# Seven products interleaved over two halves, sums left to adding transfers, and an operation's stated time changed

## The chip, the cores and the metric

The kernel runs on one core of one Trainium2 chip. The metric is the time of one execution on the device in microseconds: the median of three runs is 2280.56 us (2279.93 to 2280.93). One further execution was recorded by the hardware profiler. TensorE (PE) multiplies matrices and writes into banks of PSUM. VectorE (DVE) and ScalarE (ACT) read those banks and the on-chip memory (SBUF). GpSimd (POOL) does small work and can issue transfers (DMAs), as SyncE (SP) and ACT can.

## The reference, cut to what matters

`x` has 128 graphs of 64 nodes with 256 features, 8192 rows in all, and `adj` is 64 x 64. Four layers follow each other, each with a residual and a layer norm. The change lies in the first and in what the second needs of `adj`:

```
def layer0(x, adj, W1, W2, W3):              # 256 -> 512 -> 1024 -> 256
    conv = lambda x, W: einsum('nm,bmh->bnh', adj * adj, einsum('bnf,fh->bnh', x, W))
    return conv(relu(conv(relu(conv(x, W1)), W2)), W3)
def layer1(x, adj, W1, b1, W2, b2):
    deg = sum(adj, 0) + sum(adj, 1) - diagonal(adj)
    d = where(deg > 0, rsqrt(deg), 0)
    _, U = eigh(d[:, None] * (diag(deg) - adj) * d[None, :])
    h = relu(einsum('mn,bnd->bmd', U.T, x) @ W1 + b1)
    return einsum('nm,bmd->bnd', U, h @ W2 + b2)
x = layernorm(x + layer0(x))      # then layer1, an LSTM layer (layer 2), an attention layer (layer 3)
```

The eigenvectors U of a 64 x 64 matrix have to be there before layer 1 begins.

## The kernel before, in words

**Groups.** The rows are worked on in 16 groups of four tiles of 128 rows; `order` (L892) names which group comes when. For a group, `burst` (L1025) multiplies by adj * adj in 64 small matmuls of 64 x 64, and ACT copies the two banks out (L1037). `weigh` (L1103) multiplies one tile by the first weight into one bank, and ACT applies relu into h1. Two more bursts turn h1 into m2, and m2 times the second weight gives h2 (relu). h2 times the third weight gives s3; `mix_rows` (L1108) applies adj * adj to s3 and adds the rows x, and seven pieces of a norm per pair of tiles are queued and taken one by one at later steps.

**Seven products.** A product with the second or the third weight is split in two by two blocks and done by seven half-size products instead of eight (Winograd's form). `seven` (L1058) runs them in the order 1, 2, 6, 5, 7, 3, 4: 1, 6, 7 and 4 accumulate in one PSUM bank (`ch`), 2 in a bank of its own (`ps`), 5 and 3 in a third (`b5`). After a product ACT copies, or DVE adds and ACT applies relu, into a quarter of h2 or s3, and the next product into the same bank has to wait for that read. `step` (L1007) delays this work by one product in the written order. The products need sums of blocks of both operands. Those of the weights are made once (`sums_of_weights`, four DVE operations each). Those of m2 are made for each group by `sums_second` (L1121, four DVE operations of 128x512). Those of h2 are made by four DVE operations of 128x1024 in each group (the `VL.tensor_add` and `VL.tensor_sub` lines of `layer0`): two write the tile sh, two overwrite parts of h2. The second weight is worked off in two halves, j = 0 and j = 1, one after the other, with the next group's first burst between them. The last two groups (`PLAIN = 2`) multiply by the third weight directly (`plain`, L1093).

**Eigenvectors.** `eigen` (L275) is a Python generator that computes U beside layer 0, nearly all of it on DVE with operations of at most 64 x 64. It reduces the matrix to three diagonals in 62 steps (L382 on). Each step has some 24 DVE operations, a copy on ACT (L385), a square root on ACT (L397), and one matmul (L312), which needs DVE's copy into the tile LV, and whose result (the PSUM tile pa) DVE needs at once. Then it finds the eigenvalues by bisection (six passes, tiles Q and br, `V.least = 0.285`), evaluates continuants (tile D2, 63 pairs of operations on tw and D, `V.least = 0.22`), forms the vectors, transposes them on TensorE (L644), fixes their signs, multiplies with the reduction's matrix (pa<-AQ,Z) and lays U and its transpose out twice as u2 and ut2.

**What sets the order.** In layer 0, PE, DVE and ACT carry out instructions in the order in which Python emits them. A clock `now` advances with every matmul by its stated time. `between` (L955), called after each matmul, resumes `eigen` when `now` has reached the time that it last yielded. That time comes from `Timed` (L42), which adds a stated time for each DVE operation: `least` and 0.0009 us for each element over 64. `least` is 0.25 unless set. `soon()` asks for a return a little before DVE is free, `full()`, ahead of a matmul, at the time when it is. So stated times decide where an eigenvector matmul stands among layer 0's matmuls. What is left of `eigen` when layer 0 has been emitted is emitted at its end. Layers 1 to 3 are recorded and ordered by a planner of their own (`Plan`, shown by the profile as L162); their weights are loaded by SP into memory that layer 0 leaves.

Of the kernel before, what the change touches and what calls it, by code (L numbers as in the profile page):

```python
# [41 lines left out]
class Timed:  # L42
# [3 lines left out]
    def __init__(self, engine, free, until):  # L46
        self.engine, self.free, self.until, self.least = engine, free, until, 0.25

# [226 lines left out]
def eigen(tc, stack, a, ident, cst, u2, ut2, now, free):  # L275
# [21 lines left out]
    def ps(shape, tag):  # L297
        uid[0] += 1
        return pp.tile(shape, F32, tag=tag, name=f"{tag}_{uid[0]}")
# [5 lines left out]
    def soon():  # L305
        return max(free[0], until[0]) - 0.45

    def full(turns=0):
        return max(free[0], until[0]) + 0.6 * turns

    def mm(out, lhsT, rhs):
        PE.matmul(out, lhsT, rhs, start=True, stop=True)  # L312
        now[0] += 0.2
        until[0] = now[0] + 0.5
# [161 lines left out]
    def rows(col, n, tag):  # L476
        b = sb([N, N], "bc")
        V.tensor_scalar(b, C["ones"], col, None, op0=ALU.mult)
        yield full()
        p = ps([N, n, N], tag)  # L480
        mm(p, b, cst[:N, 0:n, :])
        return p
# [76 lines left out]
    M = cp.tile([W, FAN, HALF], F32, name="M")  # L559
    V.least = 0.285  # L560
    yield soon()
# [39 lines left out]
    V.tensor_copy(D2[:, N - 1:], dl[:, 0:1])  # L601
    V.least = 0.22
    for k in range(1, N):
# [4 lines left out]
        yield soon()  # L608
    V.least = 0.25
    D = cp.tile([N, 2, N], F32, name="D")  # L610
# [94 lines left out]
    pl = (yield from rows(lam, 1, "pa"))[:, 0, :]  # L705
    V.tensor_scalar(t0, pl, lam, 1e-12, op0=ALU.subtract, op1=ALU.add)
    V.reciprocal(t0, t0)
    V.tensor_mul(t0, t0, C["off"])
    V.tensor_copy(t1, pl)
    V.tensor_mul(t1, t1, t1)  # L710
    V.tensor_reduce(co_[8], t1, AX.X, ALU.max)
    V.tensor_scalar(co_[8], co_[8], nrm, (8.0 * 2.0 ** -24) ** 2, op0=ALU.mult, op1=ALU.mult)
    pp_ = (yield from rows(co_[7], 1, "pa"))[:, 0, :]
    rowdot(hs, pp_, t0)
    V.tensor_scalar(hs, hs, -1.0, 1.0, op0=ALU.mult, op1=ALU.add)
    V.tensor_mul(hs, hs, hs)
    V.tensor_mul(hs, hs, co_[8])
    yield soon()
    V.tensor_scalar(co_[9], s1, s1, 2.0, op0=ALU.mult, op1=ALU.mult)
    V.tensor_tensor(co_[9], co_[9], hs, ALU.is_gt)  # L720
    V.tensor_scalar(co_[10], s2e, s2e, 2.0, op0=ALU.mult, op1=ALU.mult)
    V.tensor_tensor(co_[10], co_[10], co_[8], ALU.is_gt)
    yield soon()
    V.tensor_scalar(co_[11], s2e, 0.0, -2.0, op0=ALU.is_gt, op1=ALU.mult)
    V.tensor_scalar(co_[11], co_[11], co_[10], 1.0, op0=ALU.mult, op1=ALU.add)
    V.tensor_scalar(co_[12], s1, 0.0, -2.0, op0=ALU.is_gt, op1=ALU.mult)
    V.tensor_scalar(co_[12], co_[12], 1.0, co_[11], op0=ALU.add, op1=ALU.subtract)
    V.tensor_scalar(co_[12], co_[12], co_[9], co_[11], op0=ALU.mult, op1=ALU.add)
    V.tensor_mul(co_[12], co_[12], rn)

# [4 lines left out]
    UT = cp.tile([N, N], F32, name="UT")  # L735
    V.tensor_scalar(UT, pu, co_[12], None, op0=ALU.mult)
    yield full()
    pt = ps([N, N], "pa")
    PE.transpose(pt, UT, C["eye"])
    until[0] = now[0] + 0.7  # L740
    U = cp.tile([N, N], F32, name="U")
    V.tensor_copy(U, pt)
    V.memset(u2, 0.0)
    V.memset(ut2, 0.0)
    yield full()
    for out, lhsT in ((u2, UT), (ut2, U)):
        p2 = ps([2 * N, N], "pa")
        for h in range(2):
            mm(p2[h * N:(h + 1) * N, :], lhsT, C["eye"])
        for h in range(2):  # L750
            V.tensor_copy(out[h * N:(h + 1) * N, h * N:(h + 1) * N], p2[h * N:(h + 1) * N, :])

# [19 lines left out]
QUADS = 1.17  # L772
PLAIN = 2

# [56 lines left out]
def kernel(  # L831
# [32 lines left out]
    def tl(pool, shape, tag, **kw):  # L864
        uid[0] += 1
        return pool.tile(shape, F32, tag=tag, name=f"{tag}_{uid[0]}", **kw)
# [110 lines left out]
    def quads(c):  # L977
        for m in (slice(0, N), slice(N, P)):
            for h, hs in enumerate((slice(0, N), slice(N, P))):
# [5 lines left out]
    D11, D12, D21, D22 = (aw3[:, r:r + 4, c:c + P] for r in (0, 4) for c in (0, P))  # L985
    tv = wa.tile([P, 4, 4, P], F32, name="tv")
    m1 = pa.tile([P, 2, 512], F32, name="m1")
    h1 = pa.tile([P, 4, 512], F32, name="h1")
    m2 = pa.tile([P, 4, 512], F32, name="m2")
    ss = pa.tile([P, 3, 2, 256], F32, name="ss")  # L990
    h2 = pa.tile([P, 8, 512], F32, name="h2")
    sh = pa.tile([P, 2, 4, 256], F32, name="sh")
    s3 = pa.tile([P, 4, D], F32, name="s3")
    A11, A12, A21, A22 = (m2[:, k:k + 2, r:r + 256] for r in (0, 256) for k in (0, 2))
    H11, H12, H21, H22 = (h2[:, c:c + 4, r:r + 256] for r in (0, 256) for c in (0, 4))


    second = ((None, B11, B21, B22, tw[:, 2], B12, tw[:, 1], tw[:, 0]),
              (None, A11, A12, ss[:, 2], A22, ss[:, 0], ss[:, 1], A21))
    third = ((None, D11, D21, D22, tv[:, 2], tv[:, 3], tv[:, 1], tv[:, 0]),  # L1000
             (None, H11, H12, H12, H22, sh[:, 0], sh[:, 1], H21))
    free = [0.0]
    VL = Timed(V, free, now)
    spare = [lambda: tl(pa, [P, D], "spare")]
    pending = []
# [10 lines left out]
    def bank(tag="ps"):  # L1016
        return tl(psa, [P, 512], tag, bufs={"ps": 4, "ch": 2, "b5": 1}[tag])

    def sums_of_weights(w, b12):
        VL.tensor_sub(w[7], w[3], b12)  # L1020
        VL.tensor_sub(w[5], b12, w[1])
        VL.tensor_sub(w[6], w[3], w[5])
        VL.tensor_sub(w[4], w[2], w[6])

    def burst(dst, src, c):  # L1025
# [31 lines left out]

    def seven(n, product, c11, c12, c21, c22, last):  # L1058

        def view(b):  # L1060
            return b[:, :2 * n].rearrange("p (i n) -> p i n", i=2)

        def add(dst, b):
            VL.tensor_add(dst, dst, b)
            if last is relu:
                relu(dst, dst)

        ch = view(bank("ch"))
        product(ch, 1, True)
        step(lambda: S.copy(c11, ch))  # L1070
        yield
        b2 = view(bank())
        product(b2, 2, True)
        step(lambda: add(c11, b2))
        yield
        product(ch, 6, False)
        step(lambda: S.copy(c12, ch))  # L1077
        yield
        b5 = view(bank("b5"))
        product(b5, 5, True)  # L1080
        step(lambda: S.copy(c22, b5))
        yield
        product(ch, 7, False)
        step(lambda: add(c22, ch))
        yield
        product(b5, 3, False)
        step(lambda: add(c12, b5))
        yield
        product(ch, 4, False)
        step(lambda: last(c21, ch))  # L1090
        yield

    def plain():  # L1093
        for t in (0, 2):
            p = bank().rearrange("p (t f) -> p t f", t=2)
            for i in range(2):
                run(p[:, i, :], [(h2[:, c, (t + i) * P:(t + i + 1) * P], aw3[:, c, :]) for c in range(8)])
                step((lambda p=p, t=t: S.copy(s3[:, t:t + 2, :], p)) if i else None)
                yield
        for _ in range(3):  # L1100
            yield
# [26 lines left out]
    def layer0():  # L1128
        n = NT // 4
        burst(m1, rows_of(order[0]), 0)  # L1130
        step()
        for t in range(4):
            weigh(t)
        step()
        sums_of_weights(second[0], B12)
        for c in (0, 2):
            burst(m2, h1, c)
        step()
        for g in range(n):
            sums_second()  # L1140
            for j in range(2):
                q = [h2[:, 4 * c + 2 * j:4 * c + 2 * j + 2, r:r + 256] for r in (0, 256) for c in (0, 1)]
                for _ in seven(256, by_second(j), *q, relu):
                    pass
                if j == 0 and g + 1 < n:
                    burst(m1, rows_of(order[g + 1]), 0)
                if j == g == 0:
                    sums_of_weights(third[0], D12)
            q = [s3[:, r:r + 2, c:c + P] for r in (0, 2) for c in (0, P)]
            w3 = seven(P, by_third, *q, S.copy) if g < n - PLAIN else plain()  # L1150
            next(w3)
            next(w3)
            if g < n - PLAIN:
                VL.tensor_add(sh[:, 0], H21, H22)
                VL.tensor_sub(sh[:, 1], sh[:, 0], H11)
            for t in range(4):
                if g + 1 < n:
                    weigh(t)
                if t == 0 and g < n - PLAIN:
                    VL.tensor_sub(H21, H11, H21)  # L1160
                    VL.tensor_sub(H12, H12, sh[:, 1])
            for _ in range(4):
                next(w3)
            if g + 1 < n:
                burst(m2, h1, 0)
            next(w3)
            if g + 1 < n:
                burst(m2, h1, 2)
            for t in (0, 2):
                mix_rows(g, t)  # L1170
        step()
# [657 lines left out]
```

## Time and profile before

| | |
|---|---|
| median of three runs | 2280.56 us |
| the profiled execution, its own time | 2277.23 us |
| its span, first to last instruction | 2275.4 us |
| TensorE busy (share of the span) | 2233.0 us (98%) |
| DVE busy | 1772.5 us (78%) |
| ACT busy | 1189.5 us (52%) |
| GpSimd busy | 137.0 us (6%) |
| layer 0, to its last matmul | 828.2 us |
| one group in layer 0 | about 49 to 50.5 us |
| DVE busy in layer 0, 310 to 360 us | 39.1 of 50 us |
| ACT busy there | 22.4 of 50 us |

A line of a timeline gives the start and the duration in us, the engine, the source line, the operation, out<-in by the program's names, and how many follow each other; in brackets stands how long the engine was idle before it and what ended that. A matmul of the program is two records in float32. A line of windows gives for a stretch each engine's busy time with its count, and at its end the TensorE clock granted (1.00 is full), the mean load of the 16 DMA engines, and GB/s.

### The profile page before, as it was taken

The page shows a single profiled execution, that of the slowest core. Times are in us where ns is not written, and L with a number is a line of the kernel's source. Part 1 is how long each engine was busy: PE and PEld are TensorE (multiplying, and loading weights), DVE is VectorE, ACT ScalarE, POOL GpSimd, SP SyncE. Part 2 cuts the span into 40 slices and gives each one's busy share as a digit, 9 for nine tenths or more (in the row PEclk, how much of TensorE's full clock was granted, in tenths as well). Part 3 has the DMA queues.
Part 4 walks back from the last instruction along what each step waited for, and adds up shares of the span by engine and source line. Part 5 has one row for each costly group of instructions (what it writes and reads, how often), then busy time and mean ns, then how long its engine had stood idle before and what let it go on. Part 6 is the DMA issues. An engine that isn't in the chain of part 4 may idle for free.

```text
span 2275.4 us, 52244 instructions
## 1 busy us (share of the span) xinstructions
PE 2233.0 (98%) x20612; PEld 1990.8 (87%) x20612; DVE 1772.5 (78%) x5868; ACT 1189.5 (52%) x2892; POOL 137.0 (6%) x315
## 2 busy tenths in 40 slices
PE   8999999999999989999999999999999999999997
PEld 6888888887788778999999999999999999999985
DVE  5888777776888879765967977977877887578977
ACT  3444444443434435665655655655656555566554
POOL 0000000000000010000100000000010010000012
PEclk9999999999999999999999999999999999999999
DMA  7000000000000031000111211211221211001331
GB/s 245 11 11 11 11 11 11 11 20 11 11 11 1 1 126 57 11 11 20 66 40 48 78 57 50 87 57 41 87 66 40 78 66 39 31 21 65 117 107 59
DMA packets 80117, 107.93 MB, mean 47 GB/s; under 512 B 23296, under 2 KB 64256, under 8 KB 79872
## 3 DMA queue, kind: packets, MB, share of 16 engines
q1 hardware_dynamic: 79520, 104.32, 14.1%
q8 instruction: 162, 2.65, 0.5%
q14 instruction: 83, 0.68, 0.1%
q10 hardware_dynamic: 352, 0.28, 0.0%
HBM read 57.64 MB, written 45.09 MB: 45 GB/s over the span
## 4 chain that ended last, share of the span: by engine, by line
PE 91%; DVE 6%; issue 1%; ACT 1%; DMA 1%; POOL 0%; SPq 0%; ACTq 0%; DVEq 0%; POOLq 0%
PE ps L162 58%; PE ch L966 14%; PE ps L966 10%; PE b L966 7%; PE ps L1031 2%; PE pa L312 1%; DVE w L162 1%; DVE D L52 1%; DVE tw L52 1%; DVE X L162 1%; DVE gates L162 0%; DVE st L162 0%; DVE v L162 0%; ACT gates L162 0%; DVE h L52 0%
## 5 line engine op out<-in xcount | busy, mean ns | idle before, releaser
L162 PE MATMUL ps<-w,wih 128*128 128x128 f32 (+2 forms) x2944 | 572.0, 298 | 0.3 <-ACT gates L162 0.3
L162 PE MATMUL ps<-w,sums 128*128 128x128 f32 (+2 forms) x3104 | 476.3, 293 | 0.1
L162 PEld LDWEIGHTS ps<-w,wih 128*128 128x128 f32 x2944 | 453.1, 191 | 26.5 <-issue 6.8
L162 PEld LDWEIGHTS ps<-w,sums 128*128 128x128 f32 x3104 | 422.7, 191 | 14.3 <-ACT gates L162 1.9
L162 ACT ACTIVATE gates<-gates,cbi 128x256 f32<-128x256 f32 (+4 forms) x736 | 314.0, 479 | 171.8 <-DVE gates L162 169.9
L162 DVE TENSOR_TENSOR gates<-gates,ps 128x512 f32<-128x512 f32 (+4 forms) x408 | 233.7, 583 | 171.1 <-PE ps L162 158.0
L162 ACT COPY gates<-ps 128x512 f32<-128x512 f32 (+4 forms) x408 | 204.2, 506 | 252.3 <-PE ps L162 245.4
L162 PE MATMUL ps<-hs,whh 128*128 128x128 f32 (+1 forms) x896 | 181.2, 284 | 0.1
L162 PE MATMUL ps<-w,whh 128*128 128x128 f32 (+1 forms) x896 | 181.2, 284 | 0.0
L162 ACT ACTIVATE gates<-ps,cbi 128x128 f32<-128x128 f32 (+2 forms) x368 | 119.5, 384 | 42.9 <-PE ps L162 42.5
L162 PEld LDWEIGHTS ps<-hs,whh 128*128 128x128 f32 x896 | 139.8, 191 | 0.3 <-DVE hs L162 0.3
L162 PEld LDWEIGHTS ps<-w,whh 128*128 128x128 f32 x896 | 139.8, 191 | 0.0
L975 ACT ACTIVATE h<-h 128x512 f32<-128x512 f32 x96 | 60.5, 630 | 150.9 <-DVE h L52 150.9
L966 PE MATMUL ch<-m,tw 128*128 128x256 f32 x512 | 124.7, 381 | 3.1 <-ACT h L1077 1.7
L966 PE MATMUL b<-ss,aw 128*128 128x256 f32 x512 | 121.9, 379 | 0.0
L966 PE MATMUL ps<-aw,m 128*128 128x512 f32 x256 | 116.0, 606 | 1.5 <-DMA aw<-in_a_w_dram 1.5
L966 PEld LDWEIGHTS ch<-m,tw 128*128 128x128 f32 x512 | 94.9, 190 | 18.6 <-DVE h L52 3.4
L966 PEld LDWEIGHTS b<-ss,aw 128*128 128x128 f32 x512 | 96.8, 190 | 12.9
L162 POOL TENSOR_SCALAR rs<-mv 128x2 f32<-128x2 f32 x96 | 23.5, 255 | 1325.1 <-DVE mv L162 1323.7
L966 PEld LDWEIGHTS ps<-aw,m 128*128 128x128 f32 x256 | 48.3, 194 | 55.7 <-issue 51.4
L1037 ACT COPY m<-ps 128x512 f32<-128x512 f32 x96 | 51.2, 587 | 75.5 <-PE ps L1031 75.0
L162 PE MATMUL ps<-hs,sums 128*128 128x128 f32 (+1 forms) x448 | 90.6, 284 | 0.0
(373 smaller groups left out, 4139.2 us busy)
## 6 DMA issues: line engine op xcount, KB each, us to landing
far<-w SPq DMA_DIRECT2D x42, 512.0 KB, 2.9
w<-far SPq DMA_DIRECT2D x168, 128.0 KB, 3.1
X<-rest SPq DMA_DIRECT2D x24, 512.0 KB, 3.3
out_dram<-X SPq DMA_DIRECT2D x64, 128.0 KB, 1.8
rest<-XA SPq DMA_DIRECT2D x12, 512.0 KB, 2.6
rest<-X SPq DMA_DIRECT2D x12, 512.0 KB, 2.8
XA<-in_x_dram SPq DMA_DIRECT2D x22, 256.0 KB, 6.9
aw<-in_a_w_dram SPq DMA_DIRECT2D x3, 1024.0 KB, 10.2
```

Source lines behind the costliest of these rows:

```text
L52: return getattr(self.engine, name)(out, *args, **kw)
L162: getattr(e, name)(*[real(x) for x in args], **{k: real(v) for k, v in kw.items()})
L312: PE.matmul(out, lhsT, rhs, start=True, stop=True)
L966: PE.matmul(out, lhsT, rhs, start=start, stop=stop, **kw)
L975: S.activation(dst, src, AF.Relu)
L1031: PE.matmul(p[h][m, k, t, :], src[hs, t, f], sqT2[hs, hs], start=True, stop=True)
L1037: S.copy(to[:, h, c:c + 2], p[h])
```

## The change

In the second weight, the two halves' seven products alternate, and the burst between the halves goes to the end of the group. The four DVE operations on h2 are gone. Instead ACT writes negated blocks into a larger tile sh (`less`), SP copies two blocks inside SBUF, and GpSimd issues five adding transfers of 512 KB in each group (`adds`). The third weight's sums get signs to fit (`signed_sums`), and its products the order 1, 2, 5, 6, 7, 3, 4 with the four `weigh` between 2 and 5. 15 groups instead of 14 use seven products for the third weight. `ps` has three banks instead of four, `b5` two instead of one. The second weight's sums are emitted after the second `weigh` at the start, and the first two bursts into m2 have a step each. `least` is 0.21 instead of 0.25 in most of `eigen`, 0.278 instead of 0.285 in the bisection; for layer 0's own DVE operations it stays at 0.25. Near `eigen`'s end some operations move: sums for the signs are done while a matmul is awaited, one multiplication replaces two, and the zeroing of u2 and ut2 and the spreading of U come earlier.

```
-        self.engine, self.free, self.until, self.least = engine, free, until, 0.25
+        self.engine, self.free, self.until, self.least = engine, free, until, 0.21
...
-    V.least = 0.285
+    V.least = 0.278
...
-    V.least = 0.22
+    V.least = 0.21
     for k in range(1, N):
...
-PLAIN = 2
...
-    tv = wa.tile([P, 4, 4, P], F32, name="tv")
+    tv = wa.tile([P, 5, 4, P], F32, name="tv")
...
-    h2 = pa.tile([P, 8, 512], F32, name="h2")
-    sh = pa.tile([P, 2, 4, 256], F32, name="sh")
+    h2 = pa.tile([P, 2, 8, 256], F32, name="h2")
+    sh = pa.tile([P, 4, 4, 256], F32, name="sh")
...
-    third = ((None, D11, D21, D22, tv[:, 2], tv[:, 3], tv[:, 1], tv[:, 0]),
-             (None, H11, H12, H12, H22, sh[:, 0], sh[:, 1], H21))
+    third = ((None, D11, D21, tv[:, 4], tv[:, 2], tv[:, 3], tv[:, 1], tv[:, 0]),
+             (None, H11, H12, sh[:, 3], H22, sh[:, 0], sh[:, 1], sh[:, 2]))
     free = [0.0]
     VL = Timed(V, free, now)
+    VL.least = 0.25
...
-        return tl(psa, [P, 512], tag, bufs={"ps": 4, "ch": 2, "b5": 1}[tag])
+        return tl(psa, [P, 512], tag, bufs={"ps": 3, "ch": 2, "b5": 2}[tag])
...
+    def signed_sums():
+        w = third[0]
+        VL.tensor_sub(w[7], D12, D22)
+        VL.tensor_sub(w[5], D12, D11)
+        VL.tensor_sub(w[6], D22, w[5])
+        VL.tensor_sub(w[4], D21, w[6])
+        VL.tensor_scalar(w[3], D22, -1.0, None, op0=ALU.mult)
+
+    def less(slot, j, c):
+        S.activation(sh[:, slot, 2 * j:2 * j + 2], h2[:, 0, 4 * c + 2 * j:4 * c + 2 * j + 2, :], AF.Identity, scale=-1.0)
+
+    def adds(out, src):
+        nc.gpsimd.dma_start(out, src, accum_op=ALU.add)
...
         for t in range(4):
             weigh(t)
+            if t == 1:
+                sums_of_weights(second[0], B12)
         step()
-        sums_of_weights(second[0], B12)
         for c in (0, 2):
             burst(m2, h1, c)
-        step()
+            step()
         for g in range(n):
+            last = g == n - 1
+            then = {} if last else {
+                (1, 1): lambda: less(2, 0, 0),
+                (0, 5): lambda: (less(2, 1, 0), nc.sync.dma_start(sh[:, 1], sh[:, 2])),
+                (1, 7): lambda: less(3, 0, 1),
+                (0, 4): lambda: (nc.sync.dma_start(sh[:, 0], H22), adds(sh[:, 1], H22)),
+                (1, 4): lambda: less(3, 1, 1),
+            }
             sums_second()
-            for j in range(2):
...
-                for _ in seven(256, by_second(j), *q, relu):
...
+            w2 = [seven(256, by_second(j), *[h2[:, r, 4 * c + 2 * j:4 * c + 2 * j + 2, :] for r in (0, 1) for c in (0, 1)],
+                        relu) for j in range(2)]
+            for j in (0, 0, 1, 0, 1, 0, 1, 0, 1, 0, 1, 0, 1, 1):
+                then.get((j, next(w2[j])), lambda: None)()
+            if g == 0:
+                signed_sums()
+                burst(m1, rows_of(order[1]), 0)
+            if last:
+                for _ in plain():
                     pass
...
-            if g < n - PLAIN:
-                VL.tensor_add(sh[:, 0], H21, H22)
-                VL.tensor_sub(sh[:, 1], sh[:, 0], H11)
...
-                if t == 0 and g < n - PLAIN:
-                    VL.tensor_sub(H21, H11, H21)
-                    VL.tensor_sub(H12, H12, sh[:, 1])
...
+            else:
+                q = [s3[:, r:r + 2, c:c + P] for r in (0, 2) for c in (0, P)]
+                w3 = seven(P, by_third, *q, S.copy, order=(1, 2, 5, 6, 7, 3, 4))
+                next(w3)
+                for slot in range(3):
+                    adds(sh[:, slot], H21)
+                adds(sh[:, 3], sh[:, 1])
+                next(w3)
+                for t in range(4):
                     weigh(t)
                 next(w3)
+                next(w3)
                 burst(m2, h1, 0)
                 next(w3)
+                next(w3)
                 burst(m2, h1, 2)
+                next(w3)
+                if g + 2 < n:
+                    burst(m1, rows_of(order[g + 2]), 0)
...
-    nc = bacc.Bacc("TRN2", target_bir_lowering=False, num_devices=1, dynamic_dma_scratch_size=1024)
+    nc = bacc.Bacc("TRN2", target_bir_lowering=False, num_devices=1, dynamic_dma_scratch_size=1536)
```

## The prediction

> **What bounds the kernel now.** I read the page first, then the chain that ended last, then layer 0's TensorE timeline from its start to its end, because the other layers' instructions keep their order on all five engines.
>
> ```profile
> span 2275.4 us, 52244 instructions
> ...
> PE 2233.0 (98%) x20612; PEld 1990.8 (87%) x20612; DVE 1772.5 (78%) x5868; ACT 1189.5 (52%) x2892; POOL 137.0 (6%) x315
> ```
>
> TensorE is busy for 98%, so work saved on VectorE (DVE) pays only where TensorE waits for it. The span leaves it 42 us without work. Layer 0 ends near 828; its waits stand at its two ends. The start, in the timeline of TensorE:
>
> ```profile
> 20.91 1.16 PE L1031 MATMUL ps<-sqT,h 64*64 64x64 f32 x64
> 25.64 3.78 PE L966 MATMUL ch<-m,aw 128*128 128x256 f32 x8 [3.57 <-ACT m L1037]
> 29.22 3.17 PE L966 MATMUL ps<-m,aw 128*128 128x256 f32 x8
> ```
>
> A product of eight such records takes 1.73 us elsewhere (302 us in, say); here the first takes 3.78 and the second 2.96 (29.42 to 32.38). The windows say why, in the third-last column, the granted clock:
>
> ```profile
> 22.00:24.00 2.00, 0.07 (x6) 0.00 (x0) 1.90 (x6) 0.00 (x0) 0.00 (x0) 1.00 1.10 350
> 26.00:28.00 2.00, 2.00 (x6) 1.55 (x6) 1.38 (x3) 0.55 (x2) 0.00 (x0) 0.50 1.09 349
> ```
>
> The wait: ACT's copies of m stand behind a square root (L397) that starts at 24.44, whose input DVE computes only after the four 1.2 us sums of the second weight (18.60 to 23.5). The end of layer 0:
>
> ```profile
> 812.19 13.98 PE L966 MATMUL ps<-aw,h 128*128 128x256 f32 x64
> 828.18 0.38 PE L1187 MATMUL ps<-adT,ones 128*128 128x128 f32 x2
> 829.99 0.33 PE L312 MATMUL pa<-AQ,Z 64*64 64x64 f32 x2 [0.95 <-DVE junk L52]
> 832.72 0.24 PE L739 MATMUL pa<-ident,UT 64*64 64x64 f32 x1 [2.40 <-DVE UT L52]
> 833.27 0.33 PE L312 MATMUL pa<-ident,UT 64*64 64x64 f32 x4 [0.31 <-DVE U L52]
> 834.16 0.37 PE L312 MATMUL pa<-ident,U 64*64 64x64 f32 x2 [0.56 <-DVE u L52]
> ```
>
> Layer 0's matmuls are done at 828.2; the eigenvectors' tail keeps TensorE until 834.2 with 0.19 + 0.95 + 2.40 + 0.31 + 0.56 = 4.4 us of waits. Then the clock is halved again:
>
> ```profile
> 834.00:838.00 4.00, 3.84 (x134) 3.77 (x135) 2.78 (x8) 1.20 (x3) 0.00 (x0) 0.58 1.03 412
> ```
>
> That loses (1 - 0.58) x 4 = 1.7 us. From 45 to 812 TensorE waits 2.5 us in all.
>
> **What the Trainium skill says.** "TensorE: Matmul & The Clock Gate", part 1, has the clock fall to half after an idle window of about 3.4 us; the trace agrees (3.57 us of idleness, then 0.50). "DMA: Bandwidth & Descriptors", anatomy of the SWDGE path, prices a transfer issued from GpSimd at 2.0 us + bytes/436e3, for 512 KiB 3.2 us; no such transfer is in this trace. The same page, "SDMA does more than copy", has adding done as an elementwise reduction of two streams, without a rate. "SBUF — State Buffer", "Who interferes with whom", says DVE's two-port modes keep GpSimd from writing descriptors; GpSimd issues no DMA here, so nothing shows it.
>
> **The change part by part**, against the profiled execution: span 2275.4, execution 2277.23, and 3.3 us below the median of 2280.56, so the sum is a difference that I put on the median.
>
> *One more group by seven products.* Plain products took 13.81 us (812.36 to 826.17); seven take 7 x 1.79 (16 records each, e.g. 65 to 75 us in) = 12.53. Gain 1.3.
>
> *The start.* The weight's sums are now emitted after the second weigh and stand on DVE before the eigenvectors' zeroing, so from about 14.3 (dm ends 14.26; the last piece of aw2 landed about 10.2 after its issue at 3.7) to 19.3. The four copies of m are split: the first two stand before the root. TensorE should start product 1 near 22.9: the bursts end at 22.1, plus 0.8, since with three banks instead of four the second burst's last bank must first be copied out of the first burst. The root follows about 24, the other two copies by 25.3, product 2 at 25.4, a wait of 0.8. Before, product 2 began at 29.42; 4.0 earlier, plus 1.2 for its full clock, is 5.2; I take 5.0. At worst (DVE late) 2; at best all of 3.57 + 2.05 + 1.23 = 6.9.
>
> *DVE's third-weight sums.* In 14 groups four sums of 1.21 to 1.23 us leave DVE: 68 us, worth nothing by itself.
>
> *ACT* gets 60 negations of 128x512 (0.63 us, as h<-h), 2.5 us in each of 15 groups; ACT is busy 22.5 of 50 there. Cover gone, they would delay copies, but interleaving gives a bank's next product two to three products of time where it had one.
>
> *Adding DMAs.* 75 adds on GpSimd's queue, 30 copies on SP's, 512 KB each. SP's stand ahead of the saves of rest, which nobody awaits; GpSimd's last add of a group waits for the second and holds only the next norms' roots, due 20 us later. The deadline matters. Count from the end of product 7, second half: H22 is whole at 1.9 (add 0.68, relu 0.63, hand-overs); products 4, 3, 4 end at 5.2; H21 whole at 6.2 . Product 5 of the third weight starts after two products and four weighs: 5.2 + 3.6 + 7.0 = 15.8; 6 at 17.6; 7, after a burst of 1.09, at 20.5; 3 at 22.3. Let an add hold the 16 engines r us and land 1.2 later (a store lands in 2.6 to 2.9, its transfer is 1.6), with 1.0 for descriptors (estimate): the four land at 8.4 + r, 2r, 3r, 4r. The last binds: 8.4 + 4r <= 22.3, r <= 3.5. Bounds for r:
>
> ```profile
> q1 hardware_dynamic: 79520, 104.32, 14.1%
> ...
> rest<-XA SPq DMA_DIRECT2D x12, 512.0 KB, 2.6
> ```
>
> 104.32 MB in 14.1% of 2275 us is 325 GB/s, so a plain 512 KB takes 1.6: the lower end. Two streams read make 3.2, three passes 4.8: the upper end. I take 3.2: the fourth lands at 21.2, cost 0, with 1.1 us to spare. At 4.8 it is late by 5.3, 80 us in 15 groups.
>
> *Stated times.* One step of the reduction has 24 DVE operations; in the trace it takes 6.03 less 1.01 of waiting (319.26 to 325.29), 5.02 us or 0.209 each. Stated were 0.25, a step of 6.0; now 0.21. In the written order the 62 steps end at 403 us of TensorE work instead of 531, and the last eigenvector matmul at 652 of 800 instead of at the end: three groups early. So the tail goes: 4.4 + 1.7, less about 1.1 because ACT's norms of the last group, till now hidden in it, meet layer 1's first copies, and weight loads (landing until 840.5, first sums at 845.8) lose 5 us of cover. Gain 5.0, from 2 to 6.1. The matmuls themselves only move.
> The cost: a step is now 6.3 us. A group has 7.8 of them, 39 us, plus 12 sums and adds at 0.605 and three at 0.345, 8.3: 47.5 of 49.8 us on DVE, where it was some 40. DVE waited 41.6 us in 42 steps for the eigenvector matmul; that cushion goes and TensorE will sometimes wait. A wait moves all of TensorE's later work, but not DVE's, so later steps find that cushion: the sum is DVE's largest lateness, not 62 times it. A busy ACT made DVE wait up to 1.6 us for a root (row q L397), twice that is my 3.0; 0 to 8. The bisection (0.56 us per pair of operations, stated 0.278 each) and the continuants (0.507 per pair, stated 0.21 each: 63 pairs, 5.5 us behind) meet TensorE only at the transpose L644; there the order asks 215 us of TensorE and DVE's 244 (565.3 to 809.3) less 21 (16 sums, 3 adds) less 8 of waits is the same, so the 3.0 covers it.
>
> *Interleaving.* The four waits of ch on h (2.5 us) lie between a copy and a product 1.73 us later, or behind a late DVE; the distance is now 3.5 or more. Gain 2.0, 0 to 2.5.
>
> Sum: -1.3 - 5.0 - 5.0 - 2.0 + 3.0 = -10.3: span 2265.1, median 2270.3.
>
> **Rivals.** *Late adds.* Beyond r = 3.5 TensorE stands 4(r - 3.5) us before product 3 in 15 groups; at 3.67 the whole gain is gone, and at r = 4 it is +31 - 10.3, 2301; at 4.8 2350. For it: two reads, one write and descriptors by software; against: landings of 2.6 us and 2 to 3% DMA load in this stage. 0.20. *No cushion.* Each of 62 matmuls waits 0.3 us for DVE's copy and weight load: 18.6 in place of 3.0, 2286. For it: times stated to 0.001 us of what I measure; against: the argument on lateness. 0.08. *Hidden anyway.* The start stalls as before, on another wait, and half the tail's gain is lost in layer 1's copies: -1.3 - 2.5 - 2.0 + 3.0, 2278. 0.06. Forecast 0.66.
>
> **How the numbers follow.** The likeliest case spans 2262 (no new waits) to 2277 (5 us at the start and end, 3 to 8 of waits). A difference under 0.2%, 4.6 us, can't be told from none. Faster takes the forecast and a little of the hidden case: 0.70; same, the rest of that and the edge of the others, 0.08; slower, late adds and no cushion, 0.22. With the no-cushion case inside, 2260 to 2290 leaves most of the late adds out, some 0.17.
>
> **What would show it.** Right: product 1 before 23.5 us, clock 1.00 from 24 to 34; no eigenvector matmul between layer 0's last one and layer 1; no wait of ch or b on a DMA into sh; waits of pa for DVE of a few us. Wrong: a line of TensorE waiting for DMA sh, most in product 3; or pa waiting dozens of times.

## The result and the profile after it

The changed kernel takes 2283.47 us (median of 20 runs, 2279.8 to 2286.55), the kernel before 2279.59 us beside it: a ratio of 1.0016, with a 95% interval from 1.0009 to 1.0023. It is slower by some 4 us, where 10 us of gain were forecast. In the profiled executions the span grows by 6.6 us. From the page of the changed kernel, the lines that answer to those of before:

```profile
span 2282.0 us, 52665 instructions
...
PE 2236.5 (98%) x20660; PEld 1993.6 (87%) x20660; DVE 1710.0 (75%) x5816; ACT 1217.1 (53%) x2954; POOL 204.1 (9%) x390
...
q0 software_dynamic: 10800, 39.33, 9.1%
...
sh<-sh POOLq DMA_DIRECT2D x15, 512.0 KB, 4.9
```

DVE has lost 62 us of work and TensorE is not better off. The adding transfers (the queue q0, and the last add of each group among the issues) are there, and no wait of TensorE for one of them stands in the changed kernel's trace. All of the loss lies in layer 0, whose last matmul (`ps<-adT,ones`, by its start here and below) now stands at 838.3 us where it stood at 828.2. The eigenvectors' tail has gone from the end, as forecast. TensorE's timeline there:

```profile
838.34 0.38 PE L1205 MATMUL ps<-adT,ones 128*128 128x128 f32 x2
838.66 0.33 PE L162 MATMUL ps<-u,X 64*64 64x64 f32 x2
839.49 2.09 PE L162 MATMUL ps<-u,X 64*64 64x64 f32 x126 [0.51 <-DVE rs_row L1206]
```

Layer 1's first product follows layer 0's last one; the eigenvectors' tail with its 4.4 us of waits is gone (their last matmul now starts at 689.6). From layer 0's last matmul to the end of the span it is 2282.0 - 838.3 = 1443.7 us, before 2275.4 - 828.2 = 1447.2: 3.5 us gained in this pair of executions.

Layer 0 lost its 10.2 us in two places. The first is one wait at the start. From DVE's timeline, then TensorE's, then a window of 4 us with the granted clock in the third-last column:

```profile
44.19 0.16 DVE L1211 TENSOR_TENSOR dbb<-dbb,dbl 128x2 f32<-128x2 f32 x1 [4.51 <-DMA dbb<-in_d_b_dram]
```

```profile
47.45 0.46 PE L312 MATMUL pa<-AQ,LV 128*128 128x128 f32 x2 [3.44 <-DVE LV L52]
47.74 4.88 PE L972 MATMUL ch<-m,tw 128*128 128x256 f32 x14
```

```profile
48.00:52.00 4.00, 4.00 (x13) 3.27 (x12) 3.78 (x21) 1.35 (x4) 0.00 (x0) 0.61 0.00 0
```

A sum of two small biases (128x2, 0.16 us), used only in a later layer and written behind layer 0, outside the part whose written order is kept, stands in DVE's order before the next reduction step. Its operands are among the last loads, behind all the rows of x, and land at 44 us; in the kernel before the same sum ran at 45.48 and waited for nothing. Everything behind it on DVE waits 4.5 us, then TensorE 3.4 us for the vector LV, then the clock falls. The Trainium skill's "Perfetto Trace Analysis", "Tensor Engine Instruction (MATMUL, LD_WEIGHTS)", notes that DVE takes its instructions strictly in order, and this is what it looks like.

The second place is every group of the reduction. The product that closes a group (`ps<-s,sqT`, called in `mix_rows`) starts as follows in the kernel before:

```profile
128.34 1.98 PE L966 MATMUL ps<-s,sqT 128*128 128x512 f32 x4
...
178.80 1.98 PE L966 MATMUL ps<-s,sqT 128*128 128x512 f32 x4
```

and in the changed kernel:

```profile
135.69 1.88 PE L972 MATMUL ps<-s,sqT 128*128 128x512 f32 x4
...
188.46 1.88 PE L972 MATMUL ps<-s,sqT 128*128 128x512 f32 x4
```

50.5 us a group before, 52.8 after, and 52.5 in the next (to 240.95). A group without eigenvector products takes 49.12 (498.27 to 547.39), and one such step adds 0.22 us, so the 1.8 us of eight steps explain 50.9; the rest is waiting. TensorE's own list of waits holds only a part of it; more is seen at the weight loads (PEld). The two lists overlap: the wait at 104.2 us, for one, stands in both. From 78 to 449 us, waits of TensorE, its weight loads and DVE in the changed kernel (total us, times, longest):

```profile
PE pa L312 <- DVE LV L52: 2.4, 5, 0.7
...
```

```profile
PEld pa L312 <- ACT spare L816: 4.5, 7, 1.1
...
PEld ch L972 <- DVE h L52: 3.5, 6, 0.8
...
PEld pa L312 <- DVE LV L52: 1.8, 7, 0.7
```

```profile
DVE junk L52 <- PE pa L312: 14.4, 22, 1.1
DVE q L52 <- ACT q L397: 13.7, 14, 1.0
...
```

The line with `spare` is a wait for several things of which the trace names one: at 104.19 us the weight load begins after DVE's copy into LV (103.89 to 104.08), when ACT has long been done. A count by the starts of TensorE's records is fuller (each start less the one before it, less what that shape usually takes): over the seven groups 7.4 us are lost at the reduction's products, 20 of the 54 being late by more than 0.04 us, and 2.7 us before layer 0's products into `ch`, most of which wait for DVE's sum in h. TensorE waits for DVE and DVE waits for TensorE, in the same groups. The kernel before has no line of TensorE at all in that window, and its DVE waited 26.6 us for the product and 7.8 for ACT's root.

### The profile page after: what moved, and what is told of

Its sections match the earlier page's. It is cut to its first block, busy times and chain, and to the rows that moved or that the text cites. A ratio compares the mean times of both kernels' runs of the same rounds, so it can differ in the third digit from the quotient of the medians.

```text
span 2282.0 us, 52665 instructions
## 1 busy us (share of the span) xinstructions
PE 2236.5 (98%) x20660; PEld 1993.6 (87%) x20660; DVE 1710.0 (75%) x5816; ACT 1217.1 (53%) x2954; POOL 204.1 (9%) x390
## 3 DMA queue, kind: packets, MB, share of 16 engines
q0 software_dynamic: 10800, 39.33, 9.1%
## 4 chain that ended last, share of the span: by engine, by line
PE 85%; DVE 10%; DMA 2%; issue 1%; ACT 1%; SPq 1%; POOL 1%; ACTq 0%; DVEq 0%; POOLq 0%
PE ps L162 57%; PE ch L972 12%; PE ps L972 9%; PE b L972 5%; PE ps L1052 2%; DVE q L52 1%; DVE w L162 1%; DMA XA<-in_x_dram 1%; DVE D L52 1%; DVE h L52 1%; DVE gates L162 1%; PE pa L312 1%; DVE X L162 1%; DVE xr L52 1%; DVE junk L52 1%
## 5 line engine op out<-in xcount | busy, mean ns | idle before, releaser
L972 PEld LDWEIGHTS ps<-aw,m 128*128 128x128 f32 x256 | 47.5, 194 | 50.8 <-issue 46.0
L162 ACT ACTIVATE gates<-c 128x256 f32<-128x256 f32 (+1 forms) x176 | 75.5, 432 | 27.4 <-DVE c L162 26.1
```

Of the source, the lines that this page charges most:

```text
L162: getattr(e, name)(*[real(x) for x in args], **{k: real(v) for k, v in kw.items()})
L972: PE.matmul(out, lhsT, rhs, start=start, stop=stop, **kw)
```

## The experiments

Two theories were held against each other. One: the stated 0.21 us an operation takes the slack from the reduction, so that TensorE is held by DVE's chain, and the small bias sum is a second, separate cost. The other: the slower groups come from the rest of the change (ACT's negations, the transfers, the interleaved order). Ratios are to the kernel before, run beside each kernel; differences in us are to its median.

### The stated times, in both kernels

The changed kernel with one number put back:

```
-        self.engine, self.free, self.until, self.least = engine, free, until, 0.21
+        self.engine, self.free, self.until, self.least = engine, free, until, 0.25
```

> The changed kernel with one number put back: 0.25 us stated for an operation of the tridiagonal reduction in place of 0.21; bisection, continuants and tail keep their new times. Theory 1 (slack): the seven groups that hold the reduction take 52 to 53 us only because DVE, at 0.209 us an operation, has no slack left and TensorE waits for each eigenvector product. Then groups two to eight go back to about 50.5 us, DVE waits for TensorE again (some 40 us in all), and the kernel gains 8 to 11 us on the changed kernel: about 2274, ratio to the kernel before 0.996 to 0.998. Theory 2 (the cost lies elsewhere: ACT's negations, the adding DMAs or the interleaved order slow the groups): group times stay at 52 to 53, the time within 2 us of the changed kernel's 2283.5.

Measured: 2274.56 us against 2279.21, ratio 0.9979 (0.9971 to 0.9987). The groups take 50.7 us, TensorE has no wait of its own from 78 to 449, and by the starts of its records seven groups lose 1.0 us at the reduction's products. DVE's wait for the product is back, its wait for ACT's root is what it was:

```profile
DVE junk L52 <- PE pa L312: 37.3, 32, 1.9
DVE q L52 <- ACT q L397: 14.5, 16, 1.5
```

The other way round, the kernel before with the new numbers alone:

```
-        self.engine, self.free, self.until, self.least = engine, free, until, 0.25
+        self.engine, self.free, self.until, self.least = engine, free, until, 0.21
...
-    V.least = 0.285
+    V.least = 0.278
...
-    V.least = 0.22
+    V.least = 0.21
...
-    V.least = 0.25
+    V.least = 0.21
...
     VL = Timed(V, free, now)
+    VL.least = 0.25
```

> The kernel before with the new stated times of the eigenvector operations alone (0.21, 0.278, 0.21, 0.21; the sums and adds keep 0.25): nothing else of the change. Theory 1 (slack): TensorE waits in the reduction's groups as in the changed kernel, and more, since DVE still has the third weight's four sums (4.9 us a group): 10 to 25 us of waits, less the 4 to 5 us of the tail that no longer ends layer 0: 5 to 20 us slower than before. Theory 2: no new waits; the tail's gain alone, 4 to 5 us faster than before.

Measured: 2301.78 us, ratio 1.0102 (1.0088 to 1.0115), 22.6 us slower, just above the range expected. From 45 to 860 us its TensorE waits like this:

```profile
PE ch L966 <- DVE h L52: 12.2, 15, 1.3
PE ch L966 <- ACT h L1078: 8.6, 12, 2.5
```

These are layer 0's own products, which wait until DVE and ACT have read the bank `ch`. The tail has gone from the end here too, by the new times alone: the last eigenvector matmul starts at 779.4, and layer 1 follows layer 0.

```profile
855.73 0.38 PE L1188 MATMUL ps<-adT,ones 128*128 128x128 f32 x2
856.88 2.10 PE L162 MATMUL ps<-u,X 64*64 64x64 f32 x128 [0.76 <-DVE rs_row L1189]
```

Together the two runs make a square. With the reduction's old time the rest of the change gains 4.6 us; with the new times it gains some 18 (from 2301.8 to 2283.5), most likely because the third weight's sums have left DVE; no run puts them back at 0.21. The new times cost 22.6 us without the rest and about 8.5 with it. The second theory falls: the rest of the change doesn't slow the groups.

### The small bias sums

The changed kernel with these lines, which stood behind layer 0 and were placed by the scheduler, written into the start of its second group:

```
+    def small_terms():
+        V.tensor_reduce(rs_col, adst, AX.X, ALU.add)
+        V.tensor_scalar(wide["c_b0"], wide["c_b0"], rs_col, None, op0=ALU.mult)
+        V.tensor_add(cbi, cbi, cbh)
+        V.tensor_add(dbb, dbb, dbl)
+        for q in (slice(0, 4), slice(6, 8)):
+            V.tensor_scalar(cbi[:, :, q], cbi[:, :, q], 0.5, None, op0=ALU.mult)
...
+            if g == 1:
+                small_terms()
             sums_second()
```

> The changed kernel with the small bias terms (sums and products of dbb, cbi, wide_c_b, which wait for loads that land at 44 us) moved in DVE's order from the first group to the start of the second. Theory 1: their wait of 4.51 us on DVE stands ahead of the reduction and costs TensorE 3.4 us and a halved clock; without it the first group ends 3 to 5 us earlier (group two starts near 78.5 in place of 82.6) and the kernel takes 2279 to 2280. Theory 2: the time only moves to the next late step, since DVE has no slack in any later step, and groups two to eight then take longer by as much: 2283.

Measured: 2279.75 us, ratio 1.0004 (0.9996 to 1.0013). The first group ends at 77.2 in place of 82.6, and layer 0's last matmul stands at 833.65 in place of 838.34; of the 5.4 us won in the first group 4.7 are kept.

> The changed kernel with both edits: 0.25 us stated in the reduction, and the small bias terms in the second group. If both costs stand for themselves, the gains add: 12 to 15 us on the changed kernel, about 2269 to 2271, 9 to 11 us faster than before, which was forecast for the change itself. If the slack of 0.25 already hides the wait for the loads, it gains no more than the edit of the stated time alone.

Measured: 2267.57 us, ratio 0.9951 (0.9937 to 0.9964), 11.6 us faster than the kernel before and faster than both kernels of this case. Its list of TensorE's waits from 45 to 810 us, whole:

```profile
PE pa L753 <- DVE u L52: 0.6, 1, 0.6
PE ps L972 <- DVE s L52: 0.5, 1, 0.5
PE ps L972 <- ACT h L981: 0.4, 1, 0.4
```

### How much slack is enough

The run with both edits, with the one number at 0.22 and at 0.23.

> As the run with both edits (small bias terms in the second group), but 0.22 us stated in the reduction in place of 0.25. If TensorE is paced by a DVE whose work per group is just too long (52.4 us against TensorE's 50.9 at 0.21), break-even is 1.5 us in some 8 steps of 24 operations, 0.008 us an operation: 0.22 lies past it, the groups go back to about 51 and nearly all of the gain is there, 2268 to 2271. If each step waits by its own latency, the waits shrink in proportion, a quarter of the 12 us between 0.21 and 0.25 per 0.01: about 2276.

> As before with 0.23 us stated in the reduction. Paced by DVE's work: the same as 0.25, 2267 to 2269, with no wait of TensorE for LV left in groups two to eight. Waits in proportion: about 2273.

Measured: 2274.19 us (0.9976, 0.9966 to 0.9986) and 2273.36 us (0.9971, 0.9960 to 0.9983). Neither expectation holds for the whole kernel, so layer 0 was cut into three stretches, by the starts of the product that closes a group (us; the last column is the start of layer 0's last such product):

| kernel | stated | end of group 1 | groups 2 to 11 | groups 12 to 16 | last |
|---|---|---|---|---|---|
| before | 0.25 | 77.9 | 506.9 | 241.6 | 826.4 |
| changed | 0.21 | 82.6 | 513.9 | 240.0 | 836.5 |
| small sums later | 0.21 | 77.2 | 514.7 | 240.0 | 831.9 |
| both, 0.22 | 0.22 | 76.0 | 509.6 | 240.6 | 826.1 |
| both, 0.23 | 0.23 | 76.1 | 508.3 | 242.6 | 826.9 |
| both | 0.25 | 75.3 | 505.9 | 239.9 | 821.1 |

In groups 2 to 11, which hold the reduction, 0.21 costs 8.7 us, 0.22 3.6 and 0.23 2.4 (the first group adds 1.9, 0.7 and 0.8). More than half goes with the first 0.01, as it should where DVE's chain per group is just too long; but the rest lingers, as it should where single steps are late though the mean is not. At 0.23 another 2.6 us are lost in groups 12 to 16, where the transposition of the eigenvectors (L644) falls elsewhere and waits 2.1 us for its vector w. That part belongs to where it falls, not to the reduction.

### The transfers and the sums that they replace

The run with both edits, with the four sums on DVE (`then`, the copies and the negations are gone):

```
-                for slot in range(3):
-                    adds(sh[:, slot], H21)
-                adds(sh[:, 3], sh[:, 1])
                 next(w3)
+                VL.tensor_add(sh[:, 0], H21, H22)
+                VL.tensor_sub(sh[:, 1], sh[:, 0], H11)
                 for t in range(4):
                     weigh(t)
+                    if t == 0:
+                        VL.tensor_sub(sh[:, 2], H21, H11)
+                        VL.tensor_sub(sh[:, 3], sh[:, 1], H12)
```

> The run with both edits, with the third weight's four sums of a group put back on DVE (1.2 us each, 4.9 us a group) in place of the 75 adding transfers, the 30 copies and ACT's 60 negations; the signs and the interleaving stay. If the transfers are hidden and DVE has slack at 0.25 us stated, the time is the same within 2 us, 2266 to 2270: the transfers buy nothing by themselves. If DVE's relief was what made the seven interleaved products fit, TensorE waits for the sums or for the eigenvector products and the kernel is 5 to 20 us slower.

Measured: 2271.77 us, ratio 0.9962 (0.9949 to 0.9974): 4 us slower than with the transfers, and not by waits in the groups, which take 50.4 to 50.5 us. Layer 0's last matmul is even 1 us earlier (821.9 to 822.9). The loss stands behind it. TensorE's timeline:

```profile
821.93 0.49 PE L1210 MATMUL ps<-adT,ones 128*128 128x128 f32 x2
...
823.52 0.27 PE L312 MATMUL pa<-ident,U 64*64 64x64 f32 x2 [0.39 <-DVE U L52]
...
828.52 5.44 PE L162 MATMUL ps<-bw,w 128*128 128x128 f32 x32 [2.80 <-issue]
```

The eigenvectors end with layer 0 again: their last matmul starts at 823.6, with the transfers at 746.6. Their own waits are 0.9 us here (0.47 and 0.39), not the 4.4 of the kernel before; the greater part of the loss is the wait of 2.80 us under "issue" (nothing that the profile shows) and the halved clock after it. The one book of stated times counts the third weight's sums too (0.25 + 0.0009 x 960 = 1.11 us each, 4.46 a group, 67 us in 15 groups). Taking them off DVE brings the eigenvectors forward by more than a group, at unchanged stated times. What that is worth behind layer 0 is less sure than the 4 us: from layer 0's last matmul to the end of the span the kernel before takes 1447.3 us and this run 1448.6, and twelve runs in which the eigenvectors end early take 1441.6 to 1447.4, the run with both edits 1443.3.

> The run with both edits, with the old stated times also for bisection (0.285), continuants (0.22) and the rest (0.25): the eigenvectors end as late as before. If the tail's gain is real, it goes: TensorE waits some 4 us for the last eigenvector products after layer 0's last matmul and its clock is halved after them: 4 to 6 us slower than with both edits, 2272 to 2274. If the eigenvectors' new times at the end cost more in layer 0's last groups (waits for w, u and h between 640 and 690 us) than the tail gains: the same or faster.

The edit puts 0.285, 0.22 and 0.25 back at the three later places. Measured: 2267.39 us, ratio 0.9944 (0.9930 to 0.9957): no difference from the run with both edits. The last eigenvector matmul starts at 753.3, 7 us later and still some 68 us before layer 0's end. So the three mended times at the later places aren't needed for the eigenvectors to end early; with the reduction at 0.25 the transfers suffice. The run of the new times in the kernel before shows that those suffice too.

With one more adding transfer of 512 KB ahead of each of the four:

```
+    extra = pa.tile([P, 4, 256], F32, name="extra")
+    nc.gpsimd.memset(extra, 0.0)
+
+    def doubled(src):
+        nc.gpsimd.dma_start(extra, src, accum_op=ALU.add)
...
                 for slot in range(3):
+                    doubled(H21)
                     adds(sh[:, slot], H21)
+                doubled(H21)
                 adds(sh[:, 3], sh[:, 1])
```

> The run with both edits, with one more adding transfer of the same size into an unused tile ahead of each of the four adds of a group that wait for H21. The traces show the last add landing about 2.2 us before the first product that reads it (218.9 and 221.05 us in the third group). If an add holds the queue 2.8 us (39.33 MB in 9.1% of the span), four more make it 11.2 us later: 9 us of TensorE waiting for sh in each of 15 groups, 2268 + 135 = 2400. If the transfers are limited by their latency and overlap on the 16 engines, less: below 2320.

Measured: 2334.06 us, ratio 1.0231 (1.0213 to 1.0250): 64 us slower than with both edits, 4.3 a group where 9 were expected. The page and the groups of its trace:

```profile
q0 software_dynamic: 19440, 70.79, 16.1%
...
L972 PE MATMUL ch<-tv,sh 128*128 128x128 f32 x480 | 71.6, 309 | 37.5 <-DMA sh<-h 37.3
```

16.1% of 2331.9 us over 135 adds is 2.8 us each, and 9.1% of 2282.0 over 75 is 2.8 too, so the time that an add takes of the 16 engines is as supposed. The number of adds ahead was not. GpSimd's timeline in the sixth group:

```profile
328.96 0.91 POOL L1047 DMA_DIRECT2D extra<-h  x1 [3.66 <-ACT q L397]
...
335.00 0.86 POOL L1047 DMA_DIRECT2D extra<-h  x1 [2.08 <-DMA extra<-h]
335.56 1.22 POOL L1050 DMA_DIRECT2D sh<-h  x1
340.02 0.87 POOL L1050 DMA_DIRECT2D sh<-sh  x1 [3.25 <-PE b L972]
342.46 0.86 POOL L1047 DMA_DIRECT2D extra<-h  x1 [1.57 <-DMA extra<-h]
351.02 0.86 POOL L1047 DMA_DIRECT2D extra<-h  x1 [7.70 <-DMA extra<-h]
```

Two of the four stand behind the last add (`sh<-sh`), since each add into `extra` waits for the one before it. Two ahead are 5.6 us. The 2.2 us to spare were read in one group; over the fifteen groups of the run with both edits the last add lands 0.04 to 2.7 us ahead of the product that reads it, 1.6 in the mean. 5.6 less 1.6 is 4.0, against the 4.3 measured. So the adds are hidden with 1.6 us to spare, less than one more add, and in one group with next to nothing.

### Interleaving, start and seventh product

The run with both edits, with the halves one after the other and the negations, copies and adds behind the data that they need:

```
-            for j in (0, 0, 1, 0, 1, 0, 1, 0, 1, 0, 1, 0, 1, 1):
+            for j in (0, 0, 0, 0, 0, 0, 0, 1, 1, 1, 1, 1, 1, 1):
```

> The run with both edits, with the two halves of the second weight's products one after the other, as before the change; the negations, copies and adds keep their place behind the data that they need. If interleaving gains what was forecast (2.0, from 0 to 2.5), TensorE waits again for ch's copies, a few us in all: 2269 to 2270. If DVE's adds and ACT's copies come late in more groups once both halves follow each other directly: 5 us and more. The adds can also come later: H22 is whole one product before the end instead of three, 3.4 us later, but its add is not the last of the queue.

Measured: 2317.79 us, ratio 1.0157 (1.0143 to 1.0171), 48 us slower than with both edits. From 78 to 873 us:

```profile
PE ch L972 <- ACT h L1096: 10.7, 12, 2.6
PE ch L972 <- DMA sh<-h: 8.1, 12, 2.3
PE b L972 <- DMA sh<-sh: 4.5, 6, 1.5
...
PE b L972 <- DMA sh<-h: 4.0, 6, 1.1
```

16.6 us of this list are transfers that come late: the first copy and add of H22 are issued one product nearer to the group's end, and the four adds queue behind them. 10.7 us more are ACT's copies of ch. The list holds only a part of the 51.5 us that layer 0 is longer in this trace. By the starts of TensorE's records 26 us more than with both edits are lost before products that read sh, and 23 before products of the second weight into `ch`. So interleaving is the condition under which the transfers are hidden, and nearly as much again is the wait for `ch`. The banks stay as in the changed kernel (three, two and two), so this isn't the old kernel's order with the old banks; why that wait is so much longer than the 2.5 us of the kernel before, no run shows.

The start put back (sums of the second weight after the fourth weigh, both bursts ahead of their copies):

```
             weigh(t)
-            if t == 1:
-                sums_of_weights(second[0], B12)
         step()
+        sums_of_weights(second[0], B12)
         for c in (0, 2):
             burst(m2, h1, c)
-            step()
+        step()
```

> The run with both edits, with the start's order put back: the second weight's sums after the fourth weigh, both bursts ahead of their copies. If the start gains what was forecast (5.0, from 2 to 6.9), the first group ends 4 to 6 us later than with both edits (75.3 us) and the kernel takes 2271 to 2274. If the 1.7 us that TensorE still waits for the second copy of m eat most of it: 1 to 2 us, 2269.

Measured: 2271.71 us, ratio 0.9960 (0.9947 to 0.9972). By the medians that is 2 us slower than with both edits, within the intervals; in the traces the first group ends 2.9 us later and layer 0's last matmul 3.8 later (826.70 to 822.90), and the span 3.6 (2269.8 to 2266.2). I take 3.8 below; a part of it, 0.9, lies in later groups, where eigenvector products fall elsewhere.

Plain products in the last two groups:

```
-            last = g == n - 1
+            last = g >= n - 2
```

(with the last group's weighs and bursts kept between the plain products).

> The run with both edits, with plain products of the third weight in the last two groups in place of the last one. Worked out in the prediction: 13.81 for plain products against 7 x 1.79 = 12.53: 1.3 us slower, 2268.9. If the fifteenth group's adds or its burst cost something there, no difference or faster.

Measured: 2271.46 us, ratio 0.9955 (0.9942 to 0.9967). Layer 0's last matmul starts 1.4 us later (824.29). The span is 4.6 later (2270.8): behind layer 0 TensorE has a wait of 1.99 us under "issue" and a halved clock after it, which the run with both edits doesn't have. The eigenvectors are long done in this run (746.2), so such a wait behind layer 0 needs no late eigenvectors.

## Why the prediction was wrong

The forecast was -10.3 us; the span grew by 6.6, the median by 3.9. Term by term, in us of span:

| step | forecast | measured | by |
|---|---|---|---|
| one more group by seven products | -1.3 | -1.4 | plain products in two groups |
| the start | -5.0 | -3.8 | start undone |
| small bias sum ahead of its load | none | +4.7 | small sums later |
| stated times, TensorE's new waits | +3.0 | +10.8 | layer 0's last matmul at 833.65 and 822.90 |
| the end of layer 0 | -5.0 | -3.5 | stretch behind layer 0 |
| interleaving | -2.0 | -0.2 | what is left of 6.6 |
| sum | -10.3 | +6.6 | |

**The stated times** are the step that failed: 3.0 us were put down for them, 10.8 were measured (9.6 where the time is put back first and the bias sum moved second; that is then worth 5.9). It had DVE at "47.5 of 49.8 us" and took the difference for slack, with the argument that a wait moves TensorE but not DVE. The 47.5 came out: in the seven groups of the changed kernel DVE's operations and the short gaps between them take 47.7 us a group. But that is work alone. A step also holds DVE's waits for the root on ACT and for its own product on TensorE. They come to 14.4 for the product in the reduction's steps, 4.8 for other eigenvector products and 13.7 for the root, 32.9 us, 4.7 a group, and together that is the 52.4 that a group takes. Work and waits always add up to the time taken; what counts is that these 4.7 were still there while TensorE waited for DVE. With 0.25 stated it was 8.3 a group, so less than half of the cushion could be used up. The root's part hardly moved (14.5 us with 0.25, 13.7 with 0.21): lateness didn't shorten this round trip to ACT. How much of the product's 14.4 is a round trip too, no run separates. The cushion of 41.6 us was read as if all of it could be used. The lateness then doesn't end at one largest value: DVE falls behind in every group and TensorE is held to its pace. The rival without a cushion had the right place but not the form: not every product waits, 20 of 54 are late, and a part of the loss stands before layer 0's own products. Spread over all 62, its 0.3 us each would have been 10.8 / 62 = 0.17.

**The start** had its gain, less 1.2 us, with the full clock from the first product on, which came at 23.78 where 22.9 was forecast and 23.5 was the mark. Product 2 came at 27.42 where 25.4 was forecast, behind a wait of 1.75 us where 0.8 was worked out:

```profile
27.21 0.38 PE L972 MATMUL ch<-m,aw 128*128 128x256 f32 x1 [1.75 <-issue]
```

In eight of the eleven runs with the new start this wait is 1.57 to 1.75 us. In the other three product 1 begins at 24.4 to 25.0, at a halved clock, hardly any wait is left, and product 2 still begins at 27.05 to 27.55, as in the others (26.71 to 27.67). So product 1 doesn't set the start of product 2; the last section says what the traces show of this wait. What the sum left out was the order behind it: the change moved a small operation on DVE, placed by the scheduler, ahead of a load that lands late. The prediction didn't look at when the operands of what moved would land. This is a second step that was missing, not mis-sized.

**The tail** was right in direction and off by 1.5 us, within the scatter of the stretch behind layer 0. It was put down to the mended times, and they do it alone (779.4 of 855.7 in the kernel before with nothing else changed); so do the sums taken off DVE (746.6 of 822.9). The prediction called those 68 us "worth nothing by itself". The runs don't bear that out: without the transfers the kernel with both edits is 4 us slower, and with the rest of the change the mended times cost 8.5 us instead of 22.6. Having both, the mended time of the reduction brings the end a further 57 us forward (746.6 to 689.6) and gains nothing by it, since the eigenvectors don't end layer 0 any more.

**The adds** were right: no wait, and 2.8 us for an add where 3.2 was taken. In the fourth group of the changed kernel the last one lands 1.1 us before its product (228.40 + 4.9 = 233.3 against 234.43), where 1.1 was worked out; over all groups it is 0.15 to 3.1 us, 1.6 in the mean. That the figures are so close is in part luck: the sum had the four adds run one behind the other, while the last one here is issued 5.4 us after the third (222.99, 228.40). The rival of late adds is what the doubled run shows. (At r = 4 it would have been 4 x 0.5 x 15 = 30 us, not 31; nothing hangs on it.)

**Interleaving** by itself is lost in the remainder, -0.2 here and, with both edits (a span 9.2 us shorter, of which 8.7 are the three other gains), -0.5; with the start taken at the 2.9 us of the first group it would be about 1 us more. Forecast was 2.0 from four waits; undone with the transfers in place it costs 48.

## What to carry to other kernels

Where two engines answer each other in a written order, a stated time that is exactly the mean of the operations is too short: the wait for each answer is part of the step, and the order needs room for it and for the bunches of other work between. Before a cushion of waits is counted as free, separate what is lateness from what is round trip. And whenever an order changes, look at what moved ahead of a load: an operation of 0.16 us at the head of an engine's queue can cost 4.7.

## What the hardware showed unexpectedly

The runs give a price for adding DMAs: 512 KB of float32 from SBUF added into SBUF take 2.8 us of the 16 engines (39.33 MB in 9.1% of 2282.0 us, and the same with 135 adds for 75), against 1.6 for a plain 512 KB. The last add of a group lands 4.9 us after its issue (median; 4.5 to 5.5 in the changed kernel), the others, which stand closer together, 6.5, where a plain copy takes 2.9. The Trainium skill's "DMA: Bandwidth & Descriptors", "SDMA does more than copy", names this operation without a rate.

A wait shorter than the 3.4 us that the skill's "TensorE: Matmul & The Clock Gate", part 1, gives was enough to halve the clock: after 2.80 us without a matmul in the run with the sums on DVE, and after a wait of 1.99 us in the run with two plain groups. The windows there, in 2 us (TensorE's busy time is the second number, the granted clock the third-last):

```profile
836.00:838.00 2.00, 0.18 (x12) 0.04 (x3) 2.00 (x5) 0.00 (x0) 0.00 (x0) 1.00 0.58 227
...
840.00:842.00 2.00, 2.00 (x28) 1.78 (x30) 1.51 (x9) 0.00 (x0) 1.47 (x4) 0.50 0.00 0
```

A gap of 1.72 us at 25 us in the run with both edits left the clock at full, and so did one of 1.95 us at 869 in the kernel before with the new times. So the gap's length alone doesn't decide; the page has its window run free of the program, which would fit, but no run here tests it.

The waits under "issue" have one thing in common. In all traces of this case TensorE has 23 of them of more than 0.4 us, and each ends 1.26 to 1.66 us after the end of a 16 KB packet of the queue that the profile's page calls `q8 instruction` (162 or 163 packets in a run; a moment of layer 0 picked at random stands so in 3% of cases). The wait of 1.75 us at the start ends at 27.21, its packet at 25.86; the wait of 2.80 ends at 828.52, its packet at 826.86. At the start and behind layer 0, up to 870 us, the 16 DMA engines are fully loaded while the packet is under way (a share of 1.02 to 1.10). So these are probably waits for TensorE's next instructions; no run here tests it.
